# The end of a layer with a product per node: row products on two engines, one ring of PSUM banks, weights prepared at the start

## The chip, the cores and the metric

The kernel runs on one core of a Trainium2 chip. The metric is the time of one execution on the device in microseconds (us). Before the change its median over three runs is 498.71 us (497.31 to 499.81).

A core has a matrix engine (TensorE, "PE" in the profile; its weight loads are "PEld"), a vector engine (VectorE, "DVE"), an engine for activations and copies (ScalarE, "ACT"), a general one (GpSimd, "POOL") and one that only issues transfers (SyncE, "SP"). The engines run their own instruction lists in order and wait for each other by semaphores. SBUF is the working memory (128 partitions). PSUM, where TensorE writes its products, has eight banks of 512 float32 columns per partition.

## The reference: four layers on one graph

Input are features `x` (3327 nodes, 64 numbers each) and a sparse weighted matrix `adj` (3327 x 3327), held dense. Each of four layers computes something with `adj`, adds the layer's input and normalizes each row (mean 0, variance 1). The change concerns the end of layer 1 and the beginning of layer 2.

Layer 1 (hyperbolic attention):

```python
x_tan = _logmap0(x, C)
left = x_tan @ att_W[:D] + att_b
right = x_tan @ att_W[D:]
adj_att = jax.nn.sigmoid(left + right.T) * adj
x_local = _logmap(x[:, None, :], x[None, :, :], C)
support_t = jnp.einsum('ij,ijd->id', adj_att, x_local)
return _proj(_expmap(x, support_t, C), C)
```

`_logmap`, `_expmap` and `_proj` are built of dot products of rows, an arctangent-like factor per pair of nodes, and a tanh and two square roots per node. Layer 2 is twice `x = tanh(concat([adj @ x, x]) @ W[k])`; layer 3 weights the last 100 neighbours of each node and multiplies by `weight`. Layer 0's arithmetic leaves, up to rounding, a scaled copy of the centred input, so the kernel begins with layer 1.

## The kernel before

The graph is padded to 26 blocks of 128 nodes. The two halves of the nodes (13 blocks each) lie above each other: in tiles "by columns" (`mT`, `riT`, `ljT`: 128 x 1664) partitions 0 to 63 hold the 64 features of the first half's nodes and 64 to 127 those of the second half's, so that one product of 128 columns serves a block of each half. In tiles "by rows" (`xc`, `x2`, `lj`: 128 x 26 x 64) a node is a partition and a block a slot; slots 0 to 11 are the first six blocks of both halves. Numbers per node are tiles of 128 x 26.

**Start (L88 to L1300).** `x` is loaded by two queues. SyncE then issues two blocks of `adj` that stay in SBUF (`keep`, L142 to L146), and after them layer 2's weights into `w2_dg` and layer 3's into `w3_dg`, the bias and the attention weights. TensorE turns `x`, multiplies by the attention weights and, between, issues products into a tile `idle` that nobody reads (L1219, L1277). A flag decides between two arms; here the first one runs (all nodes near the sphere).

**The pair loop of layer 1 (`near_sphere`)** takes 26 blocks of neighbours j for two times two chunks of 416 columns of nodes i: TensorE makes the dot products of pairs (L1400), ScalarE the arctangent (L1409) and the sigmoid (L1373), GpSimd multiplies by `adj` (L1378), VectorE joins the two (L1420 to L1424), TensorE sums over j (L1444) into `mT`. Within it the order of PE, ACT, DVE and POOL is the order of the program text (`manual_schedule`).

In the last four rounds of that loop the end is prepared. GpSimd multiplies `mT` and `riT` over the first 832 columns into `xm` (L1627) and makes numbers per node (L1630 to L1635). TensorE multiplies the first six blocks of `mT` by `all_m` (L1640): 128 columns that centre a row and drop its last feature, and two that pick the last features of the two halves. ScalarE squares that (`sq_e`, L1645) and copies the picked columns (`t_e`, L1649). After the loop VectorE makes three numbers per node (L1652 to L1654), the other half of `xm` (L1656) and sums the squares (`lpn`, L1657). `xm` shares its memory with `x2`.

**The end of layer 1 (`near_end`)**, with pools of its own in PSUM: four banks for `w`, one for `pe`, three for `pm`.

- TensorE: `pm` for blocks 6 to 12 (L1715), then `pe`, the sums of `xm` over features for all 13 blocks (L1735, two columns each), then the preparation of layer 2's weights (L1786, L1787, L1797, L1798), `pm` again for blocks 0 to 5, and products of `ljT` and `mT` with the prepared weights (`x_w`, `m_w`, L1755).
- ScalarE: squares of `pm` (L1729), copies of `pm` into `x2` (L1725), the prepared weights (L1778, L1794, L1795, L1820, L1870), the tanh and the two roots (L1819, L1852), with a load of the roots' table between (L1822), and copies of `x_w` into `lj` (L1761).
- VectorE: `gt` (L1770, L1745), sums of squares (L1773, L1774), and then some sixty operations on 128 x 26, one behind the other, from `pe` (L1781) over tanh and roots to the factors `alpha`, `beta` and `beta_c` (L1883, L1884, L1893). Between the last two come layer 2's first operand `lj = alpha * m_w + beta * lj` in five parts (L1890 to L1892), and after them `x2 = alpha * x2 + beta_c * xc` (L1897 to L1899).

**Layer 2 (`layers`, L517)** multiplies 128 x 64 pieces of `lj` with blocks of `adj`: four loaded ahead (`ready`), seven that stayed, and fifteen that SyncE loads into buffers as they come free (L218, `at_l` and `bt_l`; one buffer, `bt_l`, lies over memory of `near_end`). A block is 1664 KB.

Of the kernel before, what the change touches and what calls it, by code (L numbers as in the profile page):

```python
# [19 lines left out]
P = 128  # L20
N = 3327
NB = 26
# [60 lines left out]
def kernel(  # L83
# [62 lines left out]
    keep((NB - 1, NB - 2))  # L146

# [9 lines left out]
    with nc.allow_non_contiguous_dma(reason="two short columns"):  # L157
# [7 lines left out]
        nc.sync.dma_start(attw_sb, att_w.rearrange("(t d) o -> d (t o)", d=D))  # L165

# [136 lines left out]

    def layer_3_constants():
        nc.gpsimd.tensor_scalar(w3_dg, w3_dg, float(2**27), None, ALU.mult)

    def centred_weights(ps):

        pw = ps.tile([P, P], F32, name="pw_3")
        nc.tensor.matmul(pw, center, w3_dg, start=True, stop=True)  # L310
        nc.scalar.copy(w3_dg, pw)

# [877 lines left out]
    with tc.tile_pool(name="l1", bufs=1) as l1:  # L1190

        def l1_stat(name):
            return l1.tile([P, NB], F32, name=name)

        aa, g1, ga, xn, rxn, gs, gs2, gk, lpn, aav, gsp = (
            l1_stat(name)
            for name in ("aa", "g1", "ga", "xn", "rxn", "gs", "gs2", "gk", "lpn", "aav", "gsp")
# [11 lines left out]
        with tc.tile_pool(name="l1a", bufs=1) as l1a, tc.tile_pool(  # L1209
# [57 lines left out]
            for i, (g, n) in enumerate(turned):  # L1267
# [7 lines left out]
                if i in (0, 3):  # L1275
                    w = 2 if i else 4
                    nc.tensor.matmul(  # L1277
                        idle[:, : w * P], ident, center_4[:, :w], start=True, stop=True
                    )
            nc.scalar.activation(root, vq[:, :2], AF.Sqrt)  # L1280
            nc.scalar.activation(warm, ones, AF.Sigmoid)
            nc.vector.reciprocal(root, root)
# [19 lines left out]
        def near_sphere(mT, ljT_0, xm, sq_e, t_e):  # L1302
# [3 lines left out]
            with tc.tile_pool(name="n1", bufs=1, reuse_waits="tile") as n1, tc.tile_pool(  # L1306
# [235 lines left out]
                with tc.manual_schedule(  # L1542
# [69 lines left out]
                    for t in range(len(tiles)):  # L1612
# [12 lines left out]
                        if t == len(tiles) - 4:  # L1625
                            of = slice(0, 2 * CW)
                            nc.gpsimd.tensor_tensor(xm[:, of], mT[:, of], riT[:, of], ALU.mult)  # L1627
                            gp = nc.gpsimd

                            gp.tensor_scalar(gs, g1, MIN_NORM, ANGLE_LEAD, ALU.max, ALU.mult)  # L1630
                            gp.tensor_tensor(gk, gs, ga, ALU.mult)
                            gp.tensor_scalar(gsp, g1, -0.5, None, ALU.mult)
                            gp.tensor_tensor(gsp, gsp, gs, ALU.mult)
                            gp.tensor_tensor(gs2, gs, gs, ALU.mult)
                            gp.tensor_scalar(aav, aa, 1.0 / D, LN_EPS, ALU.mult, ALU.add)  # L1635
                        if t == len(tiles) - 3:
# [15 lines left out]
                    stt(inv_s, vq[:, 1], -0.5 / 0.9, r2[:, 1], op0=ALU.mult, op1=ALU.mult)  # L1652
                    stt(rxn, r2[:, 0], -0.5, inv_s, op0=ALU.mult, op1=ALU.mult)
                    vec(xn, aa, rxn, ALU.mult)  # L1654
                    for of in (slice(c * CW, (c + 1) * CW) for c in (2, 3)):
                        vec(xm[:, of], mT[:, of], riT[:, of], ALU.mult)  # L1656
                    nc.vector.tensor_reduce(lpn[:, :12], sq_e, axis=AX.X, op=ALU.add)  # L1657

        def near_end(mT, ljT, xm, t_e, x2):
# [4 lines left out]
            with tc.tile_pool(name="l1e", bufs=1) as l1e, tc.tile_pool(  # L1664
                name="l1w", bufs=4, space=PSUM
            ) as l1w, tc.tile_pool(name="l1t", bufs=1, space=PSUM) as l1t, tc.tile_pool(
                name="l1m", bufs=3, space=PSUM
            ) as l1m:
# [39 lines left out]

                pms = {}

                def m_and_t(g, n):

                    pm = l1m.tile([P, 3, P + 2], F32, tag="pm", name=f"pm_{g}")[:, :n]
# [17 lines left out]
                pe = l1t.tile([P, NBH, 2], F32, name="pe")  # L1731

                def p_of(first, last):
                    for k in range(first, last):
                        nc.tensor.matmul(  # L1735
                            pe[:, k], xm[:, k * P : (k + 1) * P], but_last,
                            start=True, stop=True,
                        )

                gt, q, k = st("gt"), lpn, st("k")  # L1740
                gp = st("gp")
# [7 lines left out]

                def in_bank(name):  # L1750
# [416 lines left out]
```

## Time and profile before

| | |
|---|---|
| median of three runs | 498.71 us (497.31 to 499.81) |
| the profiled execution: its time | 499.74 us |
| its span in the trace | 498.0 us, granted TensorE clock 0.981 |
| busy: PE, PEld, DVE, ACT, POOL | 480.5, 220.6, 349.2, 266.3, 196.8 us |
| pair loop of layer 1 | about 23 to 191 us |
| end of layer 1 | about 191 to 211 us |
| layer 2, first of two rounds | 205.2 to 289 us |
| DMA | 139.20 MB, mean 280 GB/s |

How to read it: times in lines of the timeline and of the chain are start and duration from the span's beginning. "L517" is a line of the kernel. `out<-in` are tile names. What stands behind `<-` in square brackets or in the waits is who ended the idle time. The chain of waits follows the work that ended last backwards through whatever released each step. A table by stage gives busy time of each engine, the share of the clock that TensorE was granted ("PEclk"), the DMA engines' busy share and GB/s. Operations of one engine overlap a little: a row's duration is longer than the distance to the next start.

### The profile page before, as it was taken

The page shows a single profiled execution, that of the slowest core. Times are in us where ns is not written, and L with a number is a line of the kernel's source. Part 1 is how long each engine was busy: PE and PEld are TensorE (multiplying, and loading weights), DVE is VectorE, ACT ScalarE, POOL GpSimd, SP SyncE. Part 2 cuts the span into 40 slices and gives each one's busy share as a digit, 9 for nine tenths or more (in the row PEclk, how much of TensorE's full clock was granted, in tenths as well). Part 3 has the DMA queues.
Part 4 walks back from the last instruction along what each step waited for, and adds up shares of the span by engine and source line. Part 5 has one row for each costly group of instructions (what it writes and reads, how often), then busy time and mean ns, then how long its engine had stood idle before and what let it go on. Part 6 is the DMA issues. An engine that isn't in the chain of part 4 may idle for free.

```text
span 498.0 us, 7739 instructions
## 1 busy us (share of the span) xinstructions
PE 480.5 (96%) x2865; PEld 220.6 (44%) x2865; DVE 349.2 (70%) x600; ACT 266.3 (53%) x376; POOL 196.8 (40%) x175
## 2 busy tenths in 40 slices
PE   8999999999999999999999999999999999999991
PEld 4733333333333338643434353333345555555551
DVE  6698888878888887995363322656238999689743
ACT  4799999999999985400000000000016876666641
POOL 4299899989999991000000000000352274000000
PEclk9799999999999998999999999999999999999996
DMA  8988988887888278899999009988987699949001
GB/s 273 379 247 281 328 274 273 272 273 259 280 274 276 77 277 314 372 397 428 424 426 384 0 17 403 427 349 334 421 333 235 222 334 387 365 150 356 17 1 42
DMA packets 34186, 139.20 MB, mean 280 GB/s; under 512 B 11231, under 2 KB 13025, under 8 KB 29019
## 3 DMA queue, kind: packets, MB, share of 16 engines
q1 hardware_dynamic: 30603, 137.41, 73.9%
q0 software_dynamic: 1248, 0.64, 0.6%
q10 hardware_dynamic: 2288, 0.57, 0.6%
q8 instruction: 24, 0.39, 0.3%
q14 instruction: 23, 0.19, 0.1%
HBM read 136.93 MB, written 1.04 MB: 277 GB/s over the span
## 4 chain that ended last, share of the span: by engine, by line
PE 80%; DVE 8%; DMA 5%; issue 1%; ACT 1%; SPq 0%; POOL 0%; DVEq 0%
PE cnt L517 26%; PE pq L1400 17%; PE acc L1444 16%; PE cnt L651 5%; PE acc L883 5%; DMA at_l<-in_adjT 3%; PE acc L900 2%; DMA ah<-in_adjT 2%; PE t L452 2%; DVE mask L368 2%; DVE w L667 1%; PE both L752 1%; PE cnt L508 1%; PE pn_l L403 1%; PE pe L1735 1%
## 5 line engine op out<-in xcount | busy, mean ns | idle before, releaser
L1378 POOL TENSOR_TENSOR sg<-sg,at 128x832 f32<-128x832 f32 x88 | 131.2, 1519 | 7.6 <-ACT sg L1373 3.1
L517 PE MATMUL cnt<-at_l,lj 128*64 128x416 f32 x496 | 90.7, 515 | 0.8 <-DMA at_l<-in_adjT 0.8
L1373 ACT ACTIVATE sg<-lb,rb 128x1664 f32<-128x1664 f32 (+1 forms) x53 | 88.0, 1661 | 0.0
L1400 PE MATMUL pq<-riT,ljT 64*128 64x416 f32 x416 | 87.2, 536 | 0.2
L1444 PE MATMUL acc<-v,lj 128*64 128x416 f32 x416 | 85.1, 525 | 0.0
L1409 ACT ACTIVATE pq<-pq 128x832 f32<-128x832 f32 x104 | 83.8, 850 | 1.7 <-issue 1.6
L630 ACT ACTIVATE x<-cnt 128x416 f32<-128x416 f32 x8 | 4.1, 517 | 144.9 <-PE cnt L517 144.9
L669 ACT ACTIVATE w<-cnt 128x416 int16<-128x416 f32 x135 | 63.9, 520 | 28.3 <-PE cnt L651 26.8
L1424 DVE SCALAR_TENSOR_TENSOR v<-pq,sg 128x832 f32<-128x832 f32 x52 | 53.3, 1025 | 18.7 <-ACT pq L1409 18.3
L464 POOL DMA_DIRECT2D t_rows<-tb x4 | 4.1, 1045 | 151.0 <-DVE tb L462 151.0
L1400 PEld LDWEIGHTS pq<-riT,ljT 64*128 64x128 f32 x416 | 35.6, 186 | 49.5 <-ACT pq L1409 30.6
L517 PEld LDWEIGHTS cnt<-at_l,lj 128*64 128x64 f32 x496 | 34.3, 137 | 50.9 <-issue 48.6
L883 PE MATMUL acc<-w,s 128*128 128x416 bf16 x208 | 53.1, 339 | 0.0
L667 DVE TENSOR_SCALAR w<-cnt 128x416 int16<-128x416 f32 x73 | 42.1, 587 | 10.7 <-PE cnt L651 8.3
L1444 PEld LDWEIGHTS acc<-v,lj 128*64 128x64 f32 x416 | 26.0, 136 | 52.2 <-issue 48.4
L517 PE MATMUL cnt<-kept,lj 128*64 128x416 f32 x224 | 41.6, 514 | 0.0
L651 PE MATMUL cnt<-mask,tri 128*128 128x416 bf16 x136 | 35.6, 339 | 2.1 <-DVE w L667 2.1
L368 DVE TENSOR_SCALAR mask<-ah 128x1664 bf16<-128x1664 f32 x34 | 36.4, 1096 | 1.0 <-DMA ah<-in_adjT 1.0
L1421 DVE SCALAR_TENSOR_TENSOR pq<-pq,sg 128x416 f32<-128x416 f32 x52 | 31.2, 600 | 1.8
L445 DVE TENSOR_SCALAR tm<-at_l 128x1664 bf16<-128x1664 f32 x16 | 15.7, 1023 | 22.8 <-PE t L452 20.9
L1420 DVE SCALAR_TENSOR_TENSOR v<-pq,sg 128x416 f32<-128x416 f32 x52 | 30.2, 580 | 0.0
L1044 POOL DMA_DIRECT2D out<-hid x2 | 1.0, 514 | 73.3 <-DVE hid L1049 73.3
(321 smaller groups left out, 525.6 us busy)
## 6 DMA issues: line engine op xcount, KB each, us to landing
at_l<-in_adjT SPq DMA_DIRECT2D x27, 1664.0 KB, 12.3
at<-in_adjT SPq DMA_DIRECT2D x44, 832.0 KB, 5.8
ah<-in_adjT SPq DMA_DIRECT2D x34, 832.0 KB, 6.6
kept<-in_adjT SPq DMA_DIRECT2D x7, 1664.0 KB, 9.6
bt_l<-in_adjT SPq DMA_DIRECT2D x6, 1664.0 KB
lb<-lf_rows SPq DMA_DIRECT2D x2, 384.0 KB
mask<-t_rows SPq DMA_DIRECT2D x34, 3.2 KB
ljT<-ljT SPq DMA_DIRECT2D x4, 128.0 KB
```

What stands on the lines that cost most here:

```text
L368: nc.vector.tensor_scalar(mask[q], ahead.pop(q), 0.0, None, ALU.not_equal)
L517: nc.tensor.matmul(acc[c][h * D : (h + 1) * D, :], hw[:, slot(jb), :], blocks[jb][:, o : o + CW], start=c not in begun, stop=last, skip_gr ...
L651: nc.tensor.matmul(cnt[c][e], tri, mask[q][:, of], start=True, stop=True, skip_group_check=True,)
L667: nc.vector.tensor_scalar(to, of, 0.0, None, ALU.max)
L669: nc.scalar.activation(to, of, AF.Relu)
L883: nc.tensor.matmul(acc[h, c][:, e, :], s12[:, slot(jb)].rearrange("p t d -> p (t d)"), ws[q, c, e], start=first, stop=last,)
L1373: nc.scalar.activation(sg[:, :, of], lbs[:, :, of], AF.Sigmoid, bias=rb[:, sl : sl + 1])
L1378: nc.gpsimd.tensor_tensor(sg[:, h, of], sg[:, h, of], at[:, h, of], ALU.mult)
L1400: nc.tensor.matmul(pq[:, h, :], ljT[h != jb // NBH][rows, of], riT[rows, ch * CW : (ch + 1) * CW], start=True, stop=True,)
L1409: nc.scalar.activation(pqs[t], pqs[t], AF.Arctan, bias=ANGLE_FIRST, scale=ANGLE_STEP)
L1424: stt(w, pq, ANGLE_REST, sg, op0=ALU.add, op1=ALU.mult)
L1444: nc.tensor.matmul(accs[cp, ci][h * D : (h + 1) * D, :], lj[:, slot(jb), :], w[:, h, :], start=(jb == orders[cp][0]), stop=(jb == orders[c ...
```

## The change

Seven edits in the first arm:

1. SyncE issues the weights' loads ahead of the two kept blocks of `adj`.
2. Both layers' prepared weights are made at the beginning of layer 1: `center @ W` for layers 2 and 3 takes the place of the second idle product, and ScalarE scales them into `w_mean` and `w3_dg`. One matrix `w_mean` serves both `ljT` and `mT`; the preparation in `near_end` is gone.
3. The first six blocks' row products no longer come from `mT * riT` and TensorE: VectorE multiplies the `pm` that exists already with `xc` into a new tile `xm_e` and reduces it (`xms`). GpSimd's 832 columns (L1627) are gone, TensorE's `pe` has seven blocks instead of 13, and VectorE's share of `xm` begins at column 768.
4. ScalarE copies those six blocks of `pm` into `x2` at once, so TensorE doesn't make them a second time.
5. The sums of `sq_e` move from VectorE to GpSimd, as a tree of six additions; `inv_s`, `rxn` and `xn` move there too.
6. In `near_end`, the squares of blocks 9 to 12 become eight operations of 64 columns with the sum as an accumulator output; blocks 6 to 8 keep one operation and a reduction on VectorE. The list of small operations is regrouped.
7. All of `near_end`'s PSUM tiles come from one ring of eight banks whose reuse waits tile by tile; a filling product follows the last `m_w`.

```diff
-    keep((NB - 1, NB - 2))
     w2_dg = const.tile([P, 4, P], F32, name="w2_dg")
...
         nc.sync.dma_start(attw_sb, att_w.rearrange("(t d) o -> d (t o)", d=D))
+    keep((NB - 1, NB - 2))
+    w_mean = const.tile([P, P], F32, name="w_mean")
...
+                if i == 3:
+                    for k, w in enumerate((w2_dg[:, 0, :], w3_dg)):
+                        nc.tensor.matmul(
+                            idle[:, k * P : (k + 1) * P], center, w, start=True, stop=True
+                        )
             nc.scalar.activation(root, vq[:, :2], AF.Sqrt)
             nc.scalar.activation(warm, ones, AF.Sigmoid)
+            nc.scalar.activation(w_mean, idle[:, :P], AF.Copy, scale=rows_63)
+            nc.scalar.activation(w3_dg, idle[:, P : 2 * P], AF.Copy, scale=float(2**27))
...
                         if t == len(tiles) - 4:
-                            of = slice(0, 2 * CW)
-                            nc.gpsimd.tensor_tensor(xm[:, of], mT[:, of], riT[:, of], ALU.mult)
...
+                            gp.tensor_scalar(gmh, g1, -0.5, None, ALU.mult)
+                            gp.tensor_tensor(gks, gk, s, ALU.mult)
+                            gp.tensor_scalar(gks, gks, -2.0, None, ALU.mult)
...
+                            gp.tensor_tensor(inv_s, vq[:, 1], r2[:, 1], ALU.mult)
+                            gp.tensor_tensor(rxn, r2[:, 0], inv_s, ALU.mult)
+                            gp.tensor_scalar(rxn, rxn, 0.25 / 0.9, None, ALU.mult)
+                            gp.tensor_tensor(xn, aa, rxn, ALU.mult)
...
+                            w = D
+                            while w > 2:
+                                w //= 2
+                                gp.tensor_tensor(
+                                    sq_e[:, :, :w], sq_e[:, :, :w], sq_e[:, :, w : 2 * w], ALU.add
+                                )
+                            gp.tensor_tensor(lpn[:, :12], sq_e[:, :, 0], sq_e[:, :, 1], ALU.add)
...
-                    for of in (slice(c * CW, (c + 1) * CW) for c in (2, 3)):
+                    vec(first(xm_e), pm[..., :P], first(xc), ALU.mult)
+                    nc.scalar.copy(first(x2), pm[..., :P])
+                    for of in (slice(6 * P, 3 * CW), slice(3 * CW, HALF)):
                         vec(xm[:, of], mT[:, of], riT[:, of], ALU.mult)
-                    nc.vector.tensor_reduce(lpn[:, :12], sq_e, axis=AX.X, op=ALU.add)
+                    nc.vector.tensor_reduce(xms[:, :12], xm_e, axis=AX.X, op=ALU.add)
...
-                name="l1w", bufs=4, space=PSUM
-            ) as l1w, tc.tile_pool(name="l1t", bufs=1, space=PSUM) as l1t, tc.tile_pool(
-                name="l1m", bufs=3, space=PSUM
-            ) as l1m:
+                name="l1w", bufs=8, space=PSUM, reuse_waits="tile"
+            ) as l1w:
...
+                def sums_of_squares(g, n):
+                    for k in range(n):
+                        for h in range(2):
+                            sl = 2 * (g + k) + h
+                            nc.scalar.activation(
+                                sqm[:, sl - 12], m_of(g)[:, k, h], AF.Square,
+                                accum_out=q[:, sl : sl + 1],
+                            )
...
+                for g, n in ((6, 3), (9, 3), (12, 1)):
+                    m_and_t(g, n)
+                pe = in_bank("pe")[:, :14].rearrange("p (n h) -> p n h", h=2)
+                for i in range(7):
+                    nc.tensor.matmul(
+                        pe[:, i], xm[:, (6 + i) * P : (7 + i) * P], but_last,
+                        start=True, stop=True,
+                    )
                 squares(6, 3)
-                squares(9, 3)
-                squares(12, 1)
+                sums_of_squares(9, 3)
+                sums_of_squares(12, 1)
+                xs = {g: in_bank(f"x_w_{g}") for g in (0, 4, 12, 8)}
+                of_four = dict(fours)
+                for g in xs:
+                    times(xs[g], ljT, w_mean, g, of_four[g])
                 vec(gt[:, :12], t_e, gk[:, :12], mul)
                 for g, n in ((6, 3), (9, 3), (12, 1)):
                     t_of(g, n)
+                vec(k[:, :12], xms[:, :12], gks[:, :12], mul)
+                vec(gta, gt, aa, mul)
+                for g, n in ((6, 3), (9, 3), (12, 1)):
+                    m_out(g, n)
+                x_out(xs[0], *fours[0])
+                vec(k[:, 12:].rearrange("p (n h) -> p n h", h=2), pe,
+                    gs[:, 12:].rearrange("p (n h) -> p n h", h=2), mul)
+                vec(h, k, gta, add)
+                vec(gp, k, gmh, mul)
+                vec(k, k, gt, add)
+                u2 = of(mul, k, h, "u2")
                 nc.vector.tensor_reduce(q[:, 12:18], sqm[:, :6], axis=AX.X, op=add)
-                nc.vector.tensor_reduce(q[:, 18:], sqm[:, 6:], axis=AX.X, op=add)
...
+                mw = {b: in_bank(f"m_w_{b}") for b in (0, 3, 1, 2)}
+                for b in mw:
+                    times(mw[b], mT, w_mean, *fours[b])
+                fill = in_bank("fill")
+                for _ in range(1):
+                    nc.tensor.matmul(fill, ident, center_4, start=True, stop=True)
...
+                ca = both(ux, 2.0, th, "ca", mul, add)
                 be = of(mul, th, g2, "be")
+                e = of(mul, th, u2, "e")
+                vec(ca, ca, th, mul)
+                stt(e, ux, 2.0, e, op0=mul, op1=add)
...
+                ck, al, alp = (
+                    both(ca, 1.0, v, name, add, mul) for v, name in ((k, "ck"), (gs, "al"), (gp, "alp"))
+                )
```

`in_bank(name)` takes the next tile of 128 x 512 from the ring. Of VectorE's list `uy`, `y2` and `y1` are gone; from the first root on it is unchanged. `beta_c` is written to `gmh` instead of `gsp`.

## The prediction

> **What bounds the kernel now.** The page gives TensorE 96% busy and the chain that ended last 80% TensorE, so I asked the chain of waits for 180 to 228 us, where the edited code runs, and after it SyncE's waits and the DMA stages of that stretch.
>
> ```profile
> 187.86 1.54 PE pq_early L1640 x12
> ...
> 190.94 1.79 PE pm L1715 x14
> 192.74 2.81 PE pe L1735 x26
> 195.55 0.02 issue
> 195.57 0.18 DVE e_k L1781
> ...
> 203.39 0.19 DVE gs L1883
> ...
> 210.70 0.11 DVE gsp L1893
> ...
> 211.79 13.94 DMA at_l<-in_adjT
> ...
> 225.77 2.31 PE cnt L517 x11
> ```
>
> To be seen: from 195.57 to 210.8 the end is set by VectorE alone (small operations on 26 columns to 203.6, then layer 2's rows). Its last one, L1893, does not release TensorE but a DMA, and TensorE takes the chain back only at 225.77.
>
> ```profile
> SPq L218 <- DVE gsp L1893: 15.3, 1, 15.3
> ```
>
> SyncE waited 15.3 us for L1893: layer 2's fifth block load writes over the memory of `l1e`, whose last reader L1893 is. Behind it stand the next loads.
>
> ```profile
> 206.00:210.00 4.00, 4.00 (x26) 1.71 (x24) 3.91 (x9) 0.00 (x0) 0.00 (x0) 1.00 0.97 413
> 210.00:214.00 4.00, 4.00 (x24) 1.58 (x22) 3.92 (x9) 0.00 (x0) 0.00 (x0) 1.00 0.62 177
> 214.00:218.00 4.00, 4.00 (x26) 1.72 (x24) 3.86 (x10) 0.00 (x0) 0.00 (x0) 1.00 1.02 433
> ```
> ```profile
> 225.77 3.01 PE L517 MATMUL cnt<-at_l,lj 128*64 128x416 f32 x16 [0.76 <-DMA at_l<-in_adjT]
> ```
>
> The last two columns of the stages are DMA share and GB/s; the single line is from TensorE's timeline. The DMA ran full to 210 us, fell to 177 GB/s while it waited, ran full again, and TensorE idled 0.76 us for a block. So the gain is what the change takes off the time of L1893, and not what it takes off TensorE: TensorE began layer 2 at 205.23 and would have begun at 204.53 had only VectorE's first rows (L1892, done at 204.50) held it.
>
> All sums are against this execution (span 498.0, its own time 499.74); the median of the runs is 498.71, 1.0 lower, and the difference found is carried over to it.
>
> **The change, part by part.**
>
> *Beginning.* Six weight loads move ahead of the two kept blocks on SyncE; each issues in 0.50 to 0.62, 3.5 in all. The kept blocks then issue by about 7.6, and 3.4 MB at the 426 GB/s of that stage take 8.0: both are here by some 16.3, and GpSimd first reads them at 20.08. Cost 0; without this cover up to 3.5. The two products that make the weights replace an idle product of the same size (0.68). ScalarE gets two copies of 128x128 (0.27 and 0.37, L1794 and L1795) in its idle 1.14 before 15.08; they read the bank that `prep_left` takes, so TensorE's 14.32 becomes about 14.7, and behind it TensorE idles 0.67 before 16.50. Between 0 and 0.2; I take 0.
>
> *End of the pair loop.* VectorE loses three small operations and gets a 128x768 product out of PSUM (0.95, like L1657's 768). It must follow ScalarE's read of the same banks (`t_e`, done at 190.30): in this trace L1745's three operations of 0.16 also take 0.54, for each waits for ScalarE's squares of its bank. So it runs 190.33 to 191.28, then 480 and 416 elements (0.66, 0.59): the row products end at 192.35 instead of 192.15. Loss 0.2 for what waits for them (ScalarE's squares, layer 2's first loads). The reduction of 768 only changes its input. GpSimd drops 1.95 (L1627) and adds five net small operations (0.22 to 0.34 each) and a tree of six adds; from its 384 elements at 1.0 (L820) and 26 at 0.24 the tree is 2.8, done at about 193.2, and `gq` needs it after 196. Cost 0; without that slack 1 or so.
>
> *TensorE.* `pe` shrinks from 26 instructions to 14: at 0.111 each it ends at 194.27 instead of 195.53. This is the largest saving on the path, 1.27.
>
> *ScalarE, the unknown.* Squares of the last four blocks become eight operations of 64 columns with an accumulator output. No row shows one; call its spacing c. Below: rows of 512, 384 and 128 follow each other after 0.47, 0.38 and 0.16, so 64 plain columns take 0.10. Above: a whole short operation of 0.24 (between 26 columns, 0.23, and 128, 0.28) and one more of the shortest (0.16, L1649), without overlap: 0.40. Between these I take 0.25, the middle, since both rows are equally near. VectorE's last L1745 operation waits behind all eight, and everything on VectorE is queued behind that one: it starts at 192.50 + 0.38 + 8c + 0.1, and three small operations later, at T = 193.3 + 8c, comes the first use of `pe`; never before 194.30. So T = 195.30 (0.10: 194.30; 0.40: 196.50), against 195.57 now. Half to all of what `pe` saves is eaten here.
>
> [...]
>
> *Small operations to the tanh.* From `pe` to `th`: 15 before, 2.08. After: also 15, but one is the reduction of 384 (0.54) that used to lie in VectorE's wait of 1.0 for `pe`. At 0.10 for an operation that needs nothing fresh and 0.22 for one that needs its neighbour, as in the rows: 2.51. Loss 0.43.
>
> *Tanh to root.* 22 become 20 with fewer neighbours that wait: root starts 2.05 instead of 2.33 after the first. Gain 0.28. ScalarE does beside it a table load (1.28), a warm-up (0.20) and copies of 512 and 128 (0.47, 0.28): 2.2, just covered; if not, 0.1. After the root VectorE's list is the same, and ScalarE and TensorE have less.
>
> *Sum for L1893:* 195.57 - 195.30 - 0.43 + 0.28 = **0.12 earlier** (c at 0.10: 1.12; at 0.40: 1.08 later).
>
> *TensorE after that.* 13 blocks of x and 13 of m are 52 instructions at 0.111: from 194.2 to about 200; one filling product (0.9) to 200.9. The m products need ScalarE's copies out of the first banks (about 196.0), x's first bank 196.5: no wait. Layer 2 starts at 204.4 instead of 205.23, 0.8 earlier, and with the 0.76 (and 0.3 at 221.8) it idles now TensorE would be 1.7 ahead of the block of 225.77. It can't use this: the block comes 0.12 earlier. So **0.1 us faster**: 499.6 for this execution, **498.6** for the median.
>
> **The clock.** The granted clock is 0.50 in the stage 196 to 199, after `pe`'s 2.8 us of two-column products, 0.50 from 15.0 to 21.5 us in half-microsecond stages, and 0.54 in 489 to 492, some 2 us after the last product. New is that TensorE idles 3.5 us ahead of layer 2, and shorter low work at 192.6.
>
> [...]
>
> By the rows: half rate for one spell as at 196 to 199 (3.4) loses 1.7, which the 1.7 that TensorE is ahead covers; for a spell as at 15.0 to 21.5 it loses 3.3.
>
> **Rivals.**
> 1. *Cheap accumulator, c at 0.10 to 0.15.* L1893 is 0.9 to 1.1 earlier and the fifth load issues before the queue runs dry (166 GB/s in 210.0 to 210.5). Then the dip may go as well, at most (429 - 177) x 4 / 429 = 2.3 us. Faster by 1.0 to 2.3; I say 1.7: 497.0. For it: 64 plain columns are that short. Against: the sum has to come out of the engine. Chance 0.25.
> 2. *Dear accumulator, c at 0.35 to 0.40.* ScalarE takes the place of `pe` as what VectorE waits for: 0.7 to 1.1 slower, 499.6. Chance 0.15.
> 3. *The other side: the clock.* Half rate at layer 2's start for 6.6 us loses 3.3, of which 1.7 are covered: 1.6 slower, 500.3. It decides once half rate lasts over 3.4 us behind 204.4. For: the 0.50 from 15.0 to 21.5. Against: dense products ended it in 3.4 at 199. With rival 2 TensorE is only 0.6 ahead, and it is 2.7 slower: 501.4. Chance 0.10.
> 4. *The beginning isn't covered*, or the change moves nothing that is last: the kept blocks come after 20.08 or 24.8 (up to 2 slower, 500.7), chance 0.05.
>
> **How the numbers follow.** Forecast 0.45 (c 0.20 to 0.30: 0.5 faster to 0.3 slower, 498.2 to 499.0), rivals 0.25, 0.15, 0.10, 0.05. The runs of before spread from 497.31 to 499.81, so a median moves by some 0.5 by itself. Low: rival 1's end, 496.4; high: rival 3 and that spread, 500.8. 0.5% (2.5 us) is about what a measurement of this kernel can tell from no change: faster by more needs all of rival 1 and the spread, 0.07; slower by more needs rivals 2 and 3 together or 4, 0.08; the rest is 0.85.
>
> **What would show it.** `pe` with 14 instructions ends near 194.3; the eight squares' spacing gives c; the first VectorE operation on `pe` starts at 195.3 and waits for ScalarE rather than TensorE; L1893's successor ends 0.1 earlier, and so does SyncE's wait; layer 2 starts at 204.4 and the idle time ahead of its block at 225.7 grows from 0.76 to 1.5 or so; the clock in 201 to 208 shows rival 3. I am wrong if the fifth load no longer waits for VectorE's last operation, or if something outside 186 to 226 us moves.

## The result, and the profile after

The changed kernel takes 506.12 us (median of six runs, 505.13 to 507.75), the kernel before 498.57 beside it: ratio 1.0151, 95% interval 1.0134 to 1.0168, 7.5 us slower. Its profiled execution took 505.86 (span 504.1, granted clock 0.973).

The chain of waits of the changed kernel, at the place shown of the kernel before (start, duration, what):

```profile
190.81 1.79 PE pm L1725 x14
192.60 1.46 PE pe L1774 x14
194.06 3.01 PE x_w L1762 x26
197.07 2.90 PE m_w L1762 x26
199.97 0.88 PE fill L1810 x2
200.85 10.14 issue
210.99 27.10 PE cnt L507 x144
```

TensorE is done with everything by 200.85, as forecast, and then does nothing for 10.14 us. Layer 2 starts at 210.99, not at 204.4, and 5.76 later than before. "issue" says that the profile shows no releaser for the product itself. What ended just before 210.99 stands on VectorE's timeline, its first and its last rows of `lj` and the operation behind them:

```profile
204.40 0.29 DVE L1877 TENSOR_TENSOR lj<-lj,m_w 128x128 f32<-128x128 f32 x1
...
210.20 0.69 DVE L1877 TENSOR_TENSOR lj<-lj,m_w 128x512 f32<-128x512 f32 x1
210.81 0.18 DVE L1878 SCALAR_TENSOR_TENSOR gmh<-e_n_r,e_bes 128x26 f32<-128x26 f32 x1
```

The rows that the first product multiplies were ready at 204.69. It started 0.10 after the *last* rows, at 210.89. These read `m_w`, which lies in PSUM. The allocation of the built program says where: the ring hands out bank 0 and then 7, 6, 5 and so on downwards, and the `m_w` of blocks 0, 3, 1, 2 got banks 0, 5, 7, 6. Layer 2's four accumulators are banks 4 to 7, and the first product goes to bank 6, that of the `m_w` that VectorE reads last. In the kernel before the four `w` tiles had banks 0 to 3.

The stages, with granted clock, DMA share and GB/s as the last columns:

```profile
200.00:204.00 4.00, 0.83 (x2) 0.01 (x1) 3.23 (x23) 2.73 (x6) 0.19 (x2) 1.00 1.00 421
...
206.00:210.00 4.00, 0.00 (x0) 0.00 (x0) 3.93 (x9) 0.00 (x0) 0.00 (x0) 0.50 1.01 429
210.00:214.00 4.00, 3.01 (x10) 1.32 (x12) 3.90 (x10) 0.00 (x0) 0.00 (x0) 0.50 0.67 180
214.00:218.00 4.00, 4.00 (x23) 1.63 (x22) 3.86 (x11) 0.00 (x0) 0.00 (x0) 0.93 0.86 343
```

The idle stretch halved the clock (0.50 from 206 to 214; 1.00 in e3, where products fill the stretch), so that layer 2's first products took 0.69 us from pair to pair instead of 0.35. A record is one instruction in the trace; a product here leaves two. Counted at the 21st record of layer 2 (208.78 before, 216.26 after) TensorE is 7.48 late: 5.76 from the start and 1.72 from the clock. It gets back 0.97 in layer 2 up to the 401st record (which moved by 6.51), where the idle time of 0.76 for a block at 225 is gone, and 0.4 behind that: the span grew by 6.1. SyncE's wait is where it was:

```profile
SPq L218 <- DVE gmh L1878: 15.0, 1, 15.0
```

It ends with VectorE's last small operation, which is 0.19 later than before, not 0.12 earlier.

### The profile page after: what moved, and what is told of

It is laid out like the page before. It is cut to its first block, busy times and chain, and to the rows that moved or that the text cites. A ratio compares the mean times of both kernels' runs of the same rounds, so it can differ in the third digit from the quotient of the medians.

```text
span 504.1 us, 7706 instructions
## 1 busy us (share of the span) xinstructions
PE 477.1 (95%) x2838; PEld 217.4 (43%) x2838; DVE 349.3 (69%) x597; ACT 266.6 (53%) x386; POOL 198.7 (39%) x185
## 4 chain that ended last, share of the span: by engine, by line
PE 89%; DVE 4%; issue 3%; DMA 1%; ACT 1%; POOL 0%; DVEq 0%
PE cnt L507 30%; PE pq L1396 16%; PE acc L1440 16%; PE cnt L641 6%; PE acc L873 6%; PE acc L890 3%; PE t L442 2%; DVE mask L358 2%; DMA x<-in_x 1%; PE both L742 1%; PE cnt L498 1%; DVE w L657 1%; PE pn_l L393 1%; PE x_w L1762 1%; PE m_w L1762 1%
## 5 line engine op out<-in xcount | busy, mean ns | idle before, releaser
L507 PE MATMUL cnt<-at_l,lj 128*64 128x416 f32 x496 | 92.3, 523 | 10.2 <-issue 10.2
L507 PEld LDWEIGHTS cnt<-at_l,lj 128*64 128x64 f32 x496 | 35.5, 139 | 61.3 <-issue 61.2
## 6 DMA issues: line engine op xcount, KB each, us to landing
at_l<-in_adjT SPq DMA_DIRECT2D x27, 1664.0 KB, 10.2
```

The costliest lines, as they stand in the source:

```text
L507: nc.tensor.matmul(acc[c][h * D : (h + 1) * D, :], hw[:, slot(jb), :], blocks[jb][:, o : o + CW], start=c not in begun, stop=last, skip_gr ...
```

## The experiments

Theory: the wait is for the bank (A), it halves the clock, and both together are the loss. Rivals: layer 2 waits for all of `lj` (B); the clock is most of it (C); another part of the change. Times are medians, each beside runs of the kernel before on the same chip.

| run | us | before | ratio, 95% interval |
|---|---|---|---|
| e1 two rings | 501.73 | 499.41 | 1.0053, 1.0033 to 1.0072 |
| e2 last rows' bank low | 502.43 | 499.41 | 1.0070, 1.0048 to 1.0092 |
| e3 filled wait | 504.36 | 499.41 | 1.0108, 1.0087 to 1.0129 |
| e4 before, `w` high | 503.65 | 499.41 | 1.0093, 1.0072 to 1.0114 |
| e5 two rings, fills | 500.56 | 499.15 | 1.0035, 1.0020 to 1.0049 |
| e6 e5, `beta_c` first | 499.02 | 499.15 | 0.9999, 0.9985 to 1.0014 |
| e7 e5, no accumulators | 501.49 | 499.15 | 1.0054, 1.0035 to 1.0072 |
| e8 e5, no tree | 501.81 | 499.15 | 1.0071, 1.0051 to 1.0092 |
| e9 before, `beta_c` early | 497.17 | 499.07 | 0.9971, 0.9959 to 0.9983 |
| e10 e6, kept blocks first | 501.09 | 499.07 | 1.0056, 1.0035 to 1.0076 |
| e11 e5, tree late, `beta_c` early | 498.77 | 499.07 | 0.9999, 0.9979 to 1.0019 |
| e12 e9, kept blocks late | 497.82 | 498.84 | 0.9992, 0.9977 to 1.0007 |
| e13 e10, no weights needed | 498.54 | 498.84 | 0.9999, 0.9981 to 1.0018 |
| e14 e6, weights late | 498.07 | 498.84 | 0.9988, 0.9974 to 1.0002 |

### e1: two rings of four banks

```diff
-                name="l1w", bufs=8, space=PSUM, reuse_waits="tile"
-            ) as l1w:
+                name="l1w", bufs=4, space=PSUM, reuse_waits="tile"
+            ) as l1w, tc.tile_pool(name="l1x", bufs=4, space=PSUM, reuse_waits="tile") as l1x:
...
-                xs = {g: in_bank(f"x_w_{g}") for g in (0, 4, 12, 8)}
+                xs = {g: in_bank(f"x_w_{g}", l1x) for g in (0, 4, 12, 8)}
```

> The changed kernel with its one ring of eight banks split into two rings of four, so that the products pm, pe and m_w lie in banks 0 to 3 and x_w and fill in banks 4 to 7; nothing else is changed. Theory A (the bank): in the changed kernel TensorE's first product of layer 2 waits from 200.85 to 210.99 because its accumulator lies in the bank of the m_w tile that VectorE reads last (until 210.89). Then here it starts with the first rows lj, which were ready at 204.68: about 204.7, before 205.23 in the kernel before, and the time falls from 506.1 to about 498.7 us. If the 3.85 us of idle from 200.85 to 204.7 are enough to bring the clock to half, it is 0.9 us a pair at first instead of 0.51, and about 500.4 us. Rival B (the rows): layer 2's product waits for all of lj, whose last operation ends at 210.89 too; then it starts at 210.9 to 211.0 again, and the time stays at 506. Rival C (the clock): most of the loss is the half clock at the start, and the start matters less; then a good part of the 7.5 us stays where the idle time is still some 4 us.

VectorE's first rows, TensorE's timeline and two stages:

```profile
204.55 0.29 DVE L1879 TENSOR_TENSOR lj<-lj,m_w 128x128 f32<-128x128 f32 x1
```
```profile
204.94 8.37 PE L507 MATMUL cnt<-at_l,lj 128*64 128x416 f32 x30 [3.29 <-issue]
```
```profile
204.00:208.00 4.00, 3.06 (x10) 1.40 (x12) 3.85 (x12) 0.00 (x0) 0.00 (x0) 0.50 1.01 429
208.00:211.00 3.00, 3.00 (x10) 1.08 (x9) 2.93 (x6) 0.00 (x0) 0.00 (x0) 0.53 0.83 351
```

Layer 2 starts 0.1 after the first rows (204.84): A, and B falls. By the ratios some 2.6 of the 7.5 us are left, about 1 more than expected with the half clock. For 3.29 us of idle time were enough for it (0.50 in 204 to 208), and the 21st record is still 2.6 behind the kernel before (211.38).

### e2: only the last rows' bank moved

```diff
-                mw = {b: in_bank(f"m_w_{b}") for b in (0, 3, 1, 2)}
+                mw = {b: in_bank(f"m_w_{b}") for b in (2, 3, 1, 0)}
```

> The changed kernel with one line different: the four m_w products are made in the order 2, 3, 1, 0 instead of 0, 3, 1, 2. In the ring that puts m_w_2, which VectorE reads last, into bank 0, and m_w_0, which it reads first (last read 206.33), into bank 6, under the accumulator of layer 2's first product; m_w_1 (last read 208.97) stays in bank 7, under that of its third pair. Theory A (the bank): the first pair starts at about 206.4, the third not before 209.0; the fifth pair comes 3.0 to 4.0 us earlier than in the changed kernel, and the time is 502 to 503 us. Rival B (the rows): the start stays at 210.9 to 211.0 and the time at 506.

In this execution all of the end is 0.9 earlier than in the changed kernel's (the pair loop ended at 189.92 instead of 190.81). TensorE's weight loads, and VectorE's reads of the two tiles under the first and the third accumulator:

```profile
205.53 0.33 PEld L507 LDWEIGHTS cnt<-at_l,lj 128*64 128x64 f32 x4 [6.42 <-issue]
...
208.15 0.47 PEld L507 LDWEIGHTS cnt<-at_l,lj 128*64 128x64 f32 x4 [0.91 <-DVE lj L1877]
```
```profile
204.91 0.55 DVE L1877 TENSOR_TENSOR lj<-lj,m_w 128x384 f32<-128x384 f32 x1
...
207.41 0.69 DVE L1877 TENSOR_TENSOR lj<-lj,m_w 128x512 f32<-128x512 f32 x1
```

Each accumulator's first weight load begins within 0.07 of the end of VectorE's last read of its own bank (205.46, 208.10). With the 0.9, that is the expected 206.4 and 209.0; the third accumulator begins with the fifth pair and not the third, since each product leaves two records and I had counted one. The wait was bank by bank. The time, 502.43, is within the expected 502 to 503.

### e3: the wait filled

```diff
-                for _ in range(1):
+                for _ in range(12):
                     nc.tensor.matmul(fill, ident, center_4, start=True, stop=True)
```

> The changed kernel with the product fill done 12 times in a row instead of once, 0.86 us each as its row in the trace has it, so that TensorE is busy until about 210.3 while it would wait. Nothing else is changed, and the wait stays. Theory A: layer 2 still starts at 211.0, but at full clock, 0.51 us a product from the first on instead of 0.9 for the first ten; the lag behind the kernel before, which grew from 5.75 to 7.49 us over these, stays at 5.75, and the time falls by about 1.7 us, to 504.4. Rival C (the clock is most of the loss): the time falls by over 4 us, to 502 or less. Rival D (the idle time cost no clock): 506 as before.

```profile
199.97 10.46 PE L1810 MATMUL fill<-both_m,ident 128*128 128x512 f32 x24
211.19 2.31 PE L507 MATMUL cnt<-at_l,lj 128*64 128x416 f32 x12 [0.75 <-PE fill L1810]
```

The start stays, the clock is 1.00, the 21st record comes 1.56 earlier from a start 0.2 later, and the time falls by 1.8 (2.1 by the ratios): the clock's part is about 1.7 of the 7.5 us, and rivals C and D fall.

### e4: the placement alone, in the kernel before

```diff
             with tc.tile_pool(name="l1e", bufs=1) as l1e, tc.tile_pool(
-                name="l1w", bufs=4, space=PSUM
-            ) as l1w, tc.tile_pool(name="l1t", bufs=1, space=PSUM) as l1t, tc.tile_pool(
-                name="l1m", bufs=3, space=PSUM
-            ) as l1m:
+                name="l1t", bufs=1, space=PSUM
+            ) as l1t, tc.tile_pool(name="l1m", bufs=3, space=PSUM) as l1m, tc.tile_pool(
+                name="l1w", bufs=4, space=PSUM
+            ) as l1w:
```

> The kernel before with one thing changed: its three pools of banks are opened in another order, so that x_w and m_w lie in banks 4 to 7 and pe and pm in banks 0 to 3. All operations are those of the kernel before, in its order. Theory A (the bank): layer 2's first product, at 205.23 in the kernel before, waits for VectorE's last rows here too, about 210.7 to 210.9, TensorE idles some 5.5 us from about 205 on, the clock falls to half, and the time goes from 498.6 to 504 to 506 us with no other part of the change. If the loss comes from another part of the change (the products' order, the accumulators, the weights made at the beginning), this kernel stays at 498.6.

```profile
206.64 0.92 PE L517 MATMUL cnt<-at_l,lj 128*64 128x416 f32 x4 [0.89 <-DVE lj L1892]
209.37 1.62 PE L517 MATMUL cnt<-at_l,lj 128*64 128x416 f32 x8 [1.82 <-DVE lj L1892]
211.30 1.97 PE L517 MATMUL cnt<-at_l,lj 128*64 128x416 f32 x10 [0.31 <-DVE gsp L1893]
```

Nothing but the banks changed, and TensorE now waits in three steps for VectorE's operations that read them: the 21st record is 3.9 later (212.72), the time 4.2 longer. It is less than expected because the first accumulator fell on the `m_w` that is read first, and beside waits of 0.89, 1.82 and 0.31 us the clock stayed at 1.00 (205 to 214).

### e5 and e6: the clock kept, and the load released

```diff
-                for _ in range(1):
+                for _ in range(4):
```
```diff
+                stt(beta_c, n_r, -0.5, bes, op0=mul, op1=mul)
                 for b, g, n in ((0, 0, 1), (0, 1, 3), (3, 12, 1), (1, 4, 4), (2, 8, 4)):
...
-                stt(beta_c, n_r, -0.5, bes, op0=mul, op1=mul)
```

> The changed kernel with the two rings of e1 and the product fill done four times instead of once, so that TensorE's idle time ahead of layer 2 shrinks from the 4.1 us of e1 to some 1.5 us. In e1 layer 2 started at 204.94, 0.3 before the kernel before, but at half clock, 0.69 us from pair to pair instead of 0.35, until 210.5; its 21st record came at 211.38, 2.6 us later than in the kernel before. Theory A2 (bank and clock are the whole loss): the start stays at about 204.9, at full clock from its first product, the 21st record at 208.5, and the time is that of the kernel before within 0.5 us: some 498.8 where the kernel before has 499.4. Rival (something else of the change costs too, such as VectorE's chain or the weights at the beginning): full clock, but the time stays 1 us or more above the kernel before. Rival (a longer run at full power costs clock later): the first ten products are fast, and the mean granted clock of the span falls below e1's 0.977.

> The kernel of e5 with one line moved: beta_c is made ahead of the loop over the rows lj instead of behind it. It is the last operation that reads the small tiles of layer 1's end, over which the fifth block of layer 2 is loaded, so that SyncE's load is released at about 204 instead of 211. The prediction's step (the end is set by this load: DMA runs dry from 210 to 214 and TensorE idles 0.76 us for a block at 225.77 in the kernel before): the DMA engines stay full from 205 to 214, no gap of TensorE is left near 225, and the time is 0.8 us or more below e5's. Rival (the load was hidden once layer 2 starts as it does now): the DMA engines are filled, but the time stays within 0.3 us of e5's. The move costs 0.1 us at layer 2's start in either case.

In e5 the clock is 1.00 from the start (205.08) and the 21st record comes at 208.60, as expected, 0.2 ahead of the kernel before. But the time is 1.4 above it: the rival with something else. The rival of a clock lost later falls: the mean clock of the span is 0.985, in e1 0.977. TensorE's timeline of e5 shows a part:

```profile
223.32 3.01 PE L507 MATMUL cnt<-at_l,lj 128*64 128x416 f32 x16 [0.88 <-DMA at_l<-in_adjT]
227.31 3.01 PE L507 MATMUL cnt<-at_l,lj 128*64 128x416 f32 x16 [0.98 <-DMA at_l<-in_adjT]
```

It is early enough now to wait for blocks twice. With `beta_c` first, both waits are gone (TensorE's timeline of e6):

```profile
222.01 5.87 PE L507 MATMUL cnt<-at_l,lj 128*64 128x416 f32 x32
```

The same stage in e5 and in e6:

```profile
211.00:214.00 3.00, 3.00 (x20) 1.54 (x18) 2.93 (x8) 0.00 (x0) 0.00 (x0) 1.00 0.59 146
```
```profile
211.00:214.00 3.00, 3.00 (x20) 1.41 (x18) 2.93 (x7) 0.00 (x0) 0.00 (x0) 1.00 1.00 426
```

e6 takes 1.5 us less, and is level with the kernel before.

### e7 and e8: two parts of VectorE's chain undone

```diff
-                sums_of_squares(9, 3)
-                sums_of_squares(12, 1)
+                squares(9, 3)
+                squares(12, 1)
...
-                nc.vector.tensor_reduce(q[:, 12:18], sqm[:, :6], axis=AX.X, op=add)
+                nc.vector.tensor_reduce(q[:, 12:], sqm, axis=AX.X, op=add)
```

> The kernel of e5 with the accumulating squares of the blocks 9 to 12 replaced by the kernel before's: two Square operations on ScalarE, and VectorE's sum taken over 14 rows at once instead of 6. It sizes the prediction's step that costs VectorE's first use of pe: 193.3 + 8 x 0.25 = 195.30, measured 195.17 with 0.20 from one accumulator to the next. If the accumulators bring what they cost in line, VectorE's first use of pe comes some 0.5 us earlier here (two operations of about 0.5 and 0.25 us instead of seven pairs in 1.4 us) and its sum takes 0.5 us more, so that tanh starts within 0.1 us of e5's; if they cost more than the sum that they save, tanh starts 0.2 us or more earlier. The time can't tell either from e5's.

From the end of the pair loop, VectorE's first use of `pe` comes after 3.99 instead of 4.38, but tanh after 7.27 instead of 7.36. The accumulators cost in line what they save behind. That e7's time is 0.9 above e5's, with intervals that overlap, is not explained by this.

e8 takes the `while` loop and the sixth addition out, and adds:

```diff
+                    nc.vector.tensor_reduce(lpn[:, :12], sq_e, axis=AX.X, op=ALU.add)
```

> The kernel of e5 with GpSimd's tree of five additions and a sixth taken out and the sum of sq_e given back to VectorE as one reduction of 12 x 64 behind that of xm_e. If the tree slows VectorE beside it (the changed kernel's second product xm, 416 elements, took 0.99 us beside it where the kernel before had 0.59), the product takes about 0.6 us here, the last row product on TensorE ends some 0.4 us earlier, and ScalarE's squares with it; VectorE's reduction of 0.9 us lies behind that of xm_e, ahead of the first use of pe by less than 1 us. If GpSimd has no part in it, the product still takes 0.9 to 1.0 us, and only VectorE's line is longer by 0.9 us.

VectorE's second product `xm`, by shape, in the changed kernel and in e8 (columns: busy us, mean ns, idle before):

```profile
L1665 DVE TENSOR_TENSOR x<-mT,riT 128x416 f32<-128x416 f32 x1 | 1.0, 991 | 0.0
```
```profile
L1658 DVE TENSOR_TENSOR x<-mT,riT 128x416 f32<-128x416 f32 x1 | 0.6, 585 | 0.0
```

The tree costs VectorE 0.4 while it runs beside it. Without it ScalarE's squares begin 0.4 earlier, but tanh comes 0.16 later, since VectorE sums 768 columns more; TensorE's fills end at 206.04, past the first rows, which adds to the time.

### e9: one line moved in the kernel before

```diff
                     vec(lj[:, sl], lj[:, sl], pt, add)
-                stt(beta_c, n_r, -0.5, bes, op0=mul, op1=mul)
+                    if g == 0:
+                        stt(beta_c, n_r, -0.5, bes, op0=mul, op1=mul)
```

> The kernel before with one line moved and no part of the change: beta_c is made behind the first of the five groups of rows lj instead of behind the last. It tests the prediction's first step by itself, that the end is set by VectorE's last small operation, which releases the fifth block's load: the load goes out at about 204.8 instead of 210.9. If that step holds, the DMA engines no longer run dry from 210 to 214, TensorE's idle time of 0.76 us at 225 is gone, layer 2 starts at 205.2 to 205.3 as before, and the time falls by at least 0.8 us, to some 497.5 to 498.3 where the kernel before has 499.1; e6 less e5, 1.5 us, is the upper end. Rival: the load was hidden, or the idle time comes back at the next block: within 0.3 us of the kernel before.

```profile
211.00:214.00 3.00, 3.00 (x20) 1.21 (x18) 2.93 (x7) 0.00 (x0) 0.00 (x0) 1.00 1.01 418
```

1.9 us faster by the medians, more than expected, and 1.4 by the ratio, with TensorE never waiting for a block in 205 to 229. By the traces 1.0 of it is in layer 2, where it runs 77.44 us from its first to its 401st record instead of 78.42; e12, with the same move, has 77.43. Another 0.8 lies behind that, and isn't shown to come from the move: e12 has none of it. This version beats both kernels.

### e10 to e14: what the beginning costs

By the traces layer 2 of e6 starts 14.0 us after the end of the pair loop and that of e9 14.3; both then run alike; yet e6 is 1.9 slower (1.4 by the ratios). In these two executions the rest lies ahead of the pair loop: its first product `pq` starts at 23.27 in e6 and at 21.65 in e9.

e10 puts `keep((NB - 1, NB - 2))` back ahead of the weights:

> The kernel of e6 with the order of the loads at the beginning undone: the two kept blocks go out ahead of the weights, as in the kernel before. In the changed kernel VectorE's sums start 1.2 us later (7.12 against 5.91), but the first product pq came at 22.96 against 23.12. If the beginning is covered, as the prediction has it, VectorE's sums move back to about 5.9 here, the first pq stays between 22.9 and 23.3 and the time within 0.5 us of e6's 499.0. If it is not covered, the first pq and the time come 0.5 us or more earlier than in e6. The other sign, a later first pq, would come from the weights, which the products at the beginning then wait for.

```profile
16.45 0.80 PE L1272 MATMUL idle<-w_dg,both_m 128*128 128x128 f32 x2 [2.53 <-DMA w_dg<-in_w]
```

2.1 slower than e6, by the other sign that was named: TensorE stands 2.53 us before the weights arrive, and its first `pq` comes at 24.80 instead of 23.27. The change's new products need the change's new order of loads.

e11 holds the tree back behind `xm`, with `beta_c` as in e9:

```diff
-                            w = D
-                            while w > 2:
...
+                    gp.tensor_copy(gks[:, 13:14], xm[:, HALF - 1 : HALF])
+                    w = D
+                    while w > 2:
```

> The kernel of e5 with two edits. beta_c is made behind the first group of rows, as in e9; and GpSimd's tree over sq_e is held back until VectorE's two products xm are done, by a copy of one column of xm in front of it. In e8, without the tree, the second product took 0.59 us instead of 0.98 and ScalarE's squares began 0.35 us earlier. If the tree costs VectorE by running beside the products, the second product takes 0.6 us here as well, tanh starts 0.2 to 0.4 us earlier than in e6 against the end of the pair loop, and the time is 498.6 to 498.9, some 0.2 to 0.4 below e6 and the kernel before. Rival: the tree then slows VectorE's sum xms (0.94 us) and the small operations behind it by as much, or ends after VectorE needs it (gq, some 5.6 us after the end of the pair loop), and tanh starts no earlier; then the time stays at e6's 499.0 or above.

The product takes 0.585 and the squares begin 0.4 earlier, but tanh comes 7.37 after the pair loop (e6: 7.36), the rival's case, although the time, 498.77, lies in the range of the other: it can't tell them apart. With two rings ScalarE then waits for `pm`: ahead of its second tile TensorE idles 0.47 for ScalarE's read of its bank, as it does in e5.

e12 is e9 with the two kept blocks behind the weights; e13 is e10 with `center` in place of both weights; e14 is e6 with this moved from the beginning to between `pe` and `x_w`:

```diff
+                pw = in_bank("pw", l1x)
+                for i, w in enumerate((w2_dg[:, 0, :], w3_dg)):
+                    nc.tensor.matmul(pw[:, i * P : (i + 1) * P], center, w, start=True, stop=True)
+                nc.scalar.activation(w_mean, pw[:, :P], AF.Copy, scale=rows_63)
+                nc.scalar.activation(w3_dg, pw[:, P : 2 * P], AF.Copy, scale=float(2**27))
```

> The kernel of e9, which has no part of the change, with the change's order of the loads at the beginning alone: the two kept blocks go out behind the weights. No operation of the beginning waits for the weights here. If a later x is what the beginning costs (VectorE's second sums starts at 7.1 to 7.4 us instead of 6.85), TensorE's first prep_left comes 0.3 us or more later, and the time 0.3 to 1.0 us above e9's 497.2. If the order of the loads is covered, the time stays within 0.3 us of it, and the 1.9 us that part e6 from e9 come from the products of the weights and what waits behind them.

> The kernel of e10 (kept blocks first) whose two products at the beginning take the matrix center instead of the two weights, so that nothing at the beginning waits for a weight; both are scaled into w_mean, and layer 3's weight is used as loaded. It leaves out the weights in x_w and m_w and the centring of layer 3's, so its output is another one; all later operations keep their number and shape. e10 was 2.1 us above e6, with TensorE's products of the weights waiting from 13.9 until 16.4. If that wait is e10's loss, the time falls by 2 us or more below e10's 501.1, to e6's 499.0 or less; and if the two products and ScalarE's two copies ahead of the branch cost nothing by themselves, it falls to e6 less the 1.9 us by which e9 is ahead, to some 497. Between 498 and 499 the operations themselves, in line ahead of the branch, cost about 1 us.

> The kernel of e6 with the beginning of the kernel before: kept blocks first, the idle product as it was, and no work on the weights there; the two products of the weights, and ScalarE's two copies, are made between the row products pe and x_w instead, where TensorE has some 4 us to spare, and fill is done three times. If the beginning is what parts e6 from e9, the time falls from 499.0 to 497.2 or less, with ScalarE's first copy of prep_left back at 15.1 to 15.6 us (17.1 in the changed kernel); the earlier start of layer 2 against the end of the pair loop, 14.0 us in e6 against 14.3 in e9, would put it at 496.9. Rival: the late weights hold up x_w and with it the rows, or ScalarE's copies hold up the tanh; then tanh starts more than 7.4 us after the end of the pair loop and the time is above e9's.

e12 is 0.65 above e9, with intervals that overlap, and the sign expected of the loads did not come: `prep_left` (TensorE's first products behind the idle ones) starts at 14.65, in e9 at 14.78. So a cost of their order is not shown. The wait for the weights is e10's loss: without it the time falls by 2.6. At 498.54, e13 is 1.4 above e9, in the band expected if the operations in line cost about 1 us. e14 gets back 1.0 of e6's 1.9. The intervals of e13 and e14 overlap e9's.

The clock is a rival in all of these comparisons. At the beginning it is at half for 6.8 us in e6 (12.9 to 19.7) and for 3.4 us in e9 (14.5 to 18.0). The time from the start of VectorE's second sum over `x` (6.85 to 7.44, as `x` arrives) to the first `pq`, in us:

| beginning | half clock for 6.8 us | for 3.4 us |
|---|---|---|
| with the change | 15.83 to 15.95 (changed kernel, e1, e3, e5 to e8, e11) | 14.44 (e2) |
| as before | 16.27, 15.53, 15.54 (before, e4, e14) | 14.35, 14.21 (e9, e12) |

At equal half clock the change's beginning takes from 0.4 us less to 0.4 more, and in the pair e2 and e9 0.1 more; with that beginning the longer half clock costs 1.4 to 1.5. So, as far as one execution of each can say, most of the 1.6 between the first `pq` of e6 and of e9 is the clock's. The long one stands in eight of nine of these executions with the change's beginning and in three of five with the old one; whether the change makes it more frequent, and so what the beginning costs on the median, is open.

## Why the prediction was wrong, point by point

- **The step that failed** is in "TensorE after that": "The m products need ScalarE's copies out of the first banks (about 196.0), x's first bank 196.5: no wait. Layer 2 starts at 204.4". It counts the waits of the products that write the ring, and not who takes the ring's banks afterwards. TensorE's work did end at 200.85 as worked out; then came 10.1 us of a wait that no part of the prediction had. e1, e2 and e4 show it.
- **Rival 3, the clock**, was right in the half rate at layer 2's start and near in price, and hidden behind the larger wait. Without that, e1 against e5 shows it: a half clock from 204.0 to 210.8 costs TensorE 2.8 us and the kernel 1.2 (0.9 by the ratios). I had 3.3 less 1.7 that is covered, 1.6.
- **"The end is set by" VectorE's last small operation** held: with the load issued 5.5 us sooner after the pair loop the kernel before gained 1.9 us (e9; 1.0 of it seen in layer 2), and with 7.0 sooner e6 gained 1.5 on e5. But I had put such a release at 1.0 to 2.3 only under rival 1 and did not see that a step of one line had it.
- **The sum for L1893**: 0.12 earlier, measured 0.19 later (0.32 counted from the end of the pair loop, which came 0.13 sooner). First use of `pe`: 195.17, forecast 195.30; with c = 0.20 instead of 0.25 but squares that began 0.2 late. The row products ended at 192.64, not 192.35: the term for the 416 columns, 0.59, was 0.99 beside GpSimd's tree (e8, e11). `pe` to `th`: 2.95, not 2.51; the reduction and what needs it took 0.39 from `gq` to `ux` where I had 0.10. Tanh to root: 2.06, forecast 2.05.
- **The beginning at 0** is neither refuted nor confirmed. The term for `prep_left` was too low: it started at 15.91 (forecast 14.7, before 14.32), and ScalarE's first copy of it at 17.09 instead of 15.08. Yet the first `pq` came at 22.96, and at 23.12 before, with 6.8 us of half clock in both executions (13.2 to 20.0 and 14.8 to 21.6). At equal half clock the traces leave at most 0.4 for it.

Together: 5.8 for the bank and 1.7 for the clock, less 1.4 that came back later, are the 6.1 by which the spans differ. The other 1.4 between the medians is not assigned. The profiled execution of the kernel before is 1.2 above the median of its six runs and that of the changed kernel 0.3 below its own; a longer half clock at the beginning is worth about as much.

## What to carry to other kernels

When tiles move to other banks, list for each the last reader and the next owner across the stage's end: in e2 each accumulator that was opened next began within 0.07 us of the last read of its own bank, and did not wait for the other banks, so order the ring so that the bank read last is not the one needed first. Then ask of the idle time that this leaves on TensorE whether it is long enough to cost the clock: here 3.29 us (e1) were, 0.89 and 1.82 us (e4) were not. And look at what the last small operation of a stage releases: moving `beta_c` by one line was worth more (1.9 us by the medians, e9) than regrouping sixty operations (0.19 later at the last of them). Before a difference of 1 us is put down to an edit, compare where and how long the clock was at half in the two executions.

## What the runs showed of the hardware

- The half clock came in spells of 3.4, 6.8 and 10.2 us. From the mean clock in stages of one microsecond: 204.3 to 214.5 in the changed kernel (10.2), 204.0 to 210.8 in e1 (6.8), 195.7 to 199.1 in the kernel before (3.4), and at the beginning, with the same code, 14.8 to 21.6 in the kernel before (6.8) and 14.5 to 18.0 in e9 (3.4). The changed kernel has 13.2 to 20.0 there (6.8). The stage 18 to 20 of the kernel before, of the changed kernel and of e9:

```profile
18.00:20.00 2.00, 2.00 (x13) 1.67 (x13) 1.75 (x3) 1.55 (x4) 0.07 (x1) 0.50 1.03 426
```
```profile
18.00:20.00 2.00, 2.00 (x12) 2.00 (x11) 2.00 (x4) 1.82 (x3) 0.00 (x0) 0.51 1.02 433
```
```profile
18.00:20.00 2.00, 2.00 (x27) 1.78 (x25) 2.00 (x4) 1.92 (x5) 0.00 (x0) 1.00 0.99 419
```

  Between the first and the last of these, with the same code, the first `pq` is 1.5 us apart (23.12, 21.65). One profiled execution can't size the beginning. In e1 the clock fell 2.4 us after the last product, in the changed kernel 3.5 (200.85 to 204.3), with TensorE idle in between. In gaps of 0.89 and 1.82 us (e4) it stayed at 1.00.
- An accumulator output showed as an instruction of its own, ACTIVATION_READ_ACCUMULATOR. ScalarE's timeline of the changed kernel:

```profile
193.30 0.23 ACT L1745 ACTIVATE sq_m<-pm 128x64 f32<-128x64 f32 x1
193.40 0.21 ACT L1745 ACTIVATION_READ_ACCUMULATOR sq_m<-pm 128x1 f32 x1
193.50 0.23 ACT L1745 ACTIVATE sq_m<-pm 128x64 f32<-128x64 f32 x1
```

  From one pair of 64 columns to the next it is 0.20 us.
- A VectorE product of 416 columns took 0.99 us beside GpSimd's additions and 0.59 without them, and the 480 columns ahead of it 0.65 in both (beside GpSimd in the changed kernel, alone in e8). GpSimd's five additions took 3.35 us there and 2.81 in e11, where they begin after that product.
